# Expert sums and their layer norm in two halves, Gelu read from PSUM banks in the last feed-forward part, and one gather issued from ScalarE

## The chip, the cores and the metric

The kernel runs on one NeuronCore of a Trainium2 chip, in float32 throughout. A core has five engines with an instruction stream each: TensorE (PE; its weight loads are shown apart as PEld), VectorE (DVE), ScalarE (ACT), GpSimd (POOL) and SyncE (SP). Each works its stream in order; semaphores order the engines among themselves. The metric is the device time of one execution in microseconds.

## The reference

Two "metaformer" layers on x of shape (4 batches, 384 channels, 32 x 32 places), so 1024 tokens of 384 numbers for each batch.

```python
# layer 0
x = x + conv0(ln_c(x))        # selective scan: 4 directions, 384 channels, 16 states, 1024 steps
t = tokens(x); t = t + moe(ln_t(t))      # 4 experts 384 -> 1536 -> 384, the best 2 for each token
# layer 1
x = x + attention(ln_c(x))    # 8 heads of 64, queries = keys = values = w
t = tokens(x); t = t + ffn(ln_t(t))      # 384 -> 1536 -> 384, weights are Kronecker products
```

Every layer norm takes away a mean and divides by a root of a variance plus an epsilon. The experts and the feed-forward part (FFN) use Gelu between their two matrix products. A token's expert outputs are added with its two gate weights.

## The kernel before

The work falls into a *scan* (`scan_layer`) and a *tail* (`tail_batch`: experts, attention, FFN). The scan goes through the 4 batches; a batch has 8 units (4 directions x 2 halves of 512 steps), a unit has 3 chunks of 128 channels. In a chunk (`chunk`) DMAs bring `dtr` and `bcs`, POOL multiplies (line 440, and 468 for half of the results), ACT takes exponentials `da` (line 449), DVE runs the recurrences (line 454) and the other products (line 461), and PE sums over states into `acc` (line 475), 16 matmuls for each chunk. While the scan works on batch b+1, the tail of batch b runs between its instructions. After the last scan unit only tails are left: the rest of batch 2's and all of batch 3's.

The tail of a batch, in order:

- `route`/`spread`: tokens are transposed (`tt_ps`, 669), the gates computed (`places`), and each normalised token is written twice into `rows`, in an order sorted by expert, with 16 indirect DMAs from POOL (line 696, called puts here).
- `experts`: 11 slots, 8 of 256 rows and then 3 of 128. `fetch` loads weights, `gather` loads the slot's rows `xs` (line 935, which waits for the puts of the batch) and transposes them. Then `h_ps` (963), ACT adds the bias with Identity from the bank (968), one wide Gelu goes over all of `hs` (971), and PE makes `y_ps` (978), which DVE adds a bias to and a DMA stores into `made`.
- `combine`: POOL builds the diagonal gate matrices `diag` (999) and gathers each token's two results with 16 indirect DMAs (1008); PE weighs and adds them (`w_ps`, 1015) for 8 groups m of 128 tokens, and DVE adds the sum to `xt` (1018). One store writes all of `xt` (1019).
- `prologue`: bn_stats and bn_aggr on DVE for each m (543, 544), 1/root of the variance for all 8 on ACT (152, 153), `less` (552, 553), 8 normalisations on ACT (1031), and for each half of the tokens transposes (`tc_ps`, 1039) and copies (1043) to `xc`.
- `attention`: projection `w_ps` (1064), its copies (1067), transposes (1073, 1076), then scores `s_ps` (1087), exponentials (1093) and weighted sums `o_acc` (1133), and the division (`bc_ps`, 1109).
- `last_layers`: output projection `o_ps` (1185, 1187), layer norm (`x_mean`, `z_ps`, `x_var`; z in 152, 153 and 1216), and the FFN in `hidden`: 6 row-tiled matmuls `h_ps` on 32 rows (1231), copied from their banks (1237), one wide Gelu (1240), then 6 column-tiled matmuls `f_acc` (1248). Two calls of `hidden` make a half; then a copy `fy` (1253), three matmuls `fo_ps` (1256), three adds (1258) and three stores (1259).

`exp_again` (line 148) loads the table for exp and ln again after each wide Gelu; the load of Gelu's table is put in by the compiler ahead of it.

Order and places: the source gives dependencies and rough priorities (`high_priority`); the order of each engine's stream is made by a planner when the program is built, from its own estimate of times, and is fixed from then on. On the chip an engine that waits holds up all that stands behind it in its stream. Most DMAs are issued from SP's stream, the puts and the gathers of `combine` from POOL's, a few from ACT's. Memory comes from `Room`: tags with a number of buffers (`k4` has 5 beside the scan and 4 for batch 3; `k12` 2 and 3; `kw` 8 and 10), and PSUM banks "o" and "p" (1 and 3; for batch 3's second layer, `WIDE_BANKS`, 2 and 6). A new tile waits until the oldest of its tag is free.

Of the kernel before, what the change touches and what calls it, by code (L numbers as in the profile page):

```python
# [11 lines left out]
AF = mybir.ActivationFunctionType  # L12
# [5 lines left out]
P = 128  # L18
B = 4
D = 384  # L20
DC = D // P
HW = 32
L = HW * HW
HF = 512
NH = L // HF
# [12 lines left out]
FC = HID // P  # L38
# [7 lines left out]
NSLOT = NFULL + NHALF  # L46
# [5 lines left out]
MB = L // P  # L52
# [6 lines left out]
KR = 32  # L59
# [29 lines left out]
WIDE_BANKS = {"o": 2, "p": 6}  # L89
# [26 lines left out]
class Body:  # L116
# [389 lines left out]
    def first_layer(self, b, room):  # L506

        self.experts(b, self.slots, room)
        with self.tc.high_priority(offset=FORWARD):
            xt, xn = self.combine(b, *self.place, room)  # L510
            return self.prologue(xt, xn, room)

    def second_layer(self, b, xc, room, between):
        att = self.attention(xc, self.sums[:, b], room)
# [18 lines left out]

        return self.x2[b].rearrange("(m p) d -> p m d", p=P)

    def stats(self, xt, eps, room):

        nc = self.nc
        st = room.tile([P, MB, 6], "st", "st")
        mv = room.tile([P, MB, 2], "mv", "mv")  # L540
        rstd = room.tile([P, MB], "rstd", "rstd")
        for m in range(MB):
            nc.vector.bn_stats(st[:, m, :], xt[:, m, :])
            nc.vector.bn_aggr(mv[:, m, :], st[:, m, :])
        self.inverse_root(rstd, mv[:, :, 1], eps)
        return mv[:, :, 0], rstd

    def less_mean(self, mean, rstd, room, tag):

        less = room.tile([P, MB], tag, "less")  # L550
        ps = room.bank("p", "less_ps")[:, :MB]
        self.nc.scalar.copy(ps, rstd)
        self.nc.vector.scalar_tensor_tensor(less, mean, -1.0, ps, op0=ALU.mult, op1=ALU.mult)
        return less
# [338 lines left out]
    def experts(self, b, routed, room):  # L893
# [38 lines left out]
        def gather(s):  # L932
            at, size = extent(s)
            xs = room.tile([P, size // P, D], "k4", "xs")
            got = nc.sync.dma_start(
                out=xs, in_=rows[at : at + size, :].rearrange("(t p) d -> p t d", p=P)
            ).ins
            for put in placed:
                self.depend(got, put)
            xc = room.tile([P, DC, size], "k4", "xc")  # L940
            for lo in range(0, DC, HF // size):
                ps = room.bank("p", "xc_ps").rearrange("p (r l) -> p r l", l=size)
                n = min(HF // size, DC - lo)
                for c in range(lo, lo + n):
                    for t in range(size // P):
                        nc.tensor.transpose(  # L946
                            ps[:, c - lo, t * P : (t + 1) * P], xs[:, t, c * P : (c + 1) * P],
                            self.ident,
                        )
                nc.vector.tensor_copy(xc[:, lo : lo + n, :], ps[:, :n, :])  # L950
            return xc

        weights, xc = fetch(0), gather(0)
        for s in range(NSLOT):
            w1, w2, bb = weights
            at, size = extent(s)
            hs = room.tile([P, FC, size], "k12", "hs")
            n = HF // size
            for f in range(0, FC, n):
                ps = room.bank("p", "h_ps").rearrange("p (r l) -> p r l", l=size)  # L960
                for r in range(n):
                    for c in range(DC):
                        nc.tensor.matmul(  # L963
                            ps[:, r, :], w1[(f + r) // wf][:, c, (f + r) % wf * P : ((f + r) % wf + 1) * P],
                            xc[:, c, :], start=(c == 0), stop=(c == DC - 1),
                        )
                for r in range(n):
                    nc.scalar.activation(  # L968
                        hs[:, f + r, :], ps[:, r, :], AF.Identity, bias=bb[:, f + r : f + r + 1]
                    )  # L970
            self.exp_again(nc.scalar.activation(hs, hs, AF.Gelu).ins)  # L971
            if s + 1 < NSLOT:
                weights, xc = fetch(s + 1), gather(s + 1)
            y = room.tile([P, size // P, D], "k4", "y")
            for t in range(size // P):
                out = room.bank("o", "y_ps")
                for f in range(FC):
                    nc.tensor.matmul(  # L978
                        out[:, :D], hs[:, f, t * P : (t + 1) * P], w2[f // wf][:, f % wf, :],
                        start=(f == 0), stop=(f == FC - 1),  # L980
                    )
                nc.vector.tensor_add(y[:, t, :], out[:, :D], bb[:, FC:])  # L982

            queue = nc.sync if s + 1 < NSLOT else nc.scalar
            queue.dma_start(
                out=made[at : at + size, :].rearrange("(t p) d -> p t d", p=P), in_=y
            )

    def combine(self, b, pos, gate, room):
# [15 lines left out]
        for m in range(MB):  # L1005
            got.append(room.tile([P, TOP, D], "kw", "got"))
            for k in range(TOP):
# [4 lines left out]
        for m in range(MB):  # L1012
            ps = room.bank("p", "w_ps")[:, :D]
            for k in range(TOP):
                nc.tensor.matmul(
                    ps, diag[k][:, m, :], got[m][:, k, :], start=(k == 0), stop=(k == TOP - 1)
                )
            nc.vector.tensor_add(xt[:, m, :], xt[:, m, :], ps)
        nc.sync.dma_start(out=self.tokens(b), in_=xt)
        return xt, [got[m][:, 0, :] for m in range(MB)]  # L1020

    def prologue(self, xt, xn, room):


        nc = self.nc
        mean, rstd = self.stats(xt, self.eps6, room)
        less = self.less_mean(mean, rstd, room, "less")
        for m in range(MB):  # L1030
            nc.scalar.activation(
                xn[m], xt[:, m, :], AF.Identity, bias=less[:, m : m + 1], scale=rstd[:, m : m + 1]
            )
        xc = room.tile([P, DC, L], "k12", "xc")
        for i in range(NH):
            for c in range(DC):
                ps = room.bank("p", "tc_ps")
                for j in range(HF // P):
                    nc.tensor.transpose(
                        ps[:, j * P : (j + 1) * P], xn[i * (HF // P) + j][:, c * P : (c + 1) * P],  # L1040
                        self.ident,
                    )
                nc.scalar.copy(xc[:, c, halves(i)], ps)
        return xc
# [101 lines left out]
    def last_layers(self, b, att, room, between=()):  # L1146
# [24 lines left out]
        )  # L1171

        x2 = room.tile([P, DC, L], "k12", "x2")
        zs = []
        for i in range(NH):
            part = []
            for m in range(i * (HF // P), (i + 1) * (HF // P), 2):
# [36 lines left out]
            z = room.tile([P, HF], "k4", "z")  # L1214
            self.inverse_root(z, var, self.eps5, scale=1.0 / D)
            nc.vector.tensor_mul(z, z, zp)
            zs.append(z)
# [279 lines left out]
```

## Time and profile before

| what | us |
|---|---|
| median of 3 runs | 4267.21 (4253.81 to 4271.01) |
| the profiled execution, its own time | 4260.96 |
| its span, first to last instruction | 4258.3 |
| busy: PE, POOL, DVE, ACT | 3330.8, 3020.0, 2838.3, 2519.7 |
| last scan matmul (line 475) of batches 0, 1, 2, 3 ends at | 760, 1654, 2543, 3426 |
| first `h_ps` of the last FFN to the last add (1258) | 4187.8 to 4251.7 |

A timeline row holds start, duration, engine, line, operation, out<-in, shapes and count; in brackets stand the engine's idle time before it and what ended that. One float32 matmul leaves two records in PE's rows, so "x12" are 6 matmuls. A stretch's row holds its length, the busy time and count for each of PE, PEld, DVE, ACT and POOL, the granted share of PE's full clock, the busy share of the DMA engines, and GB/s.

### The profile page before, as it was taken

The numbers are of one execution on the slowest core, as the hardware profiler recorded it, in microseconds if no ns is written. First come the engines' busy times: TensorE is split into PE (matmuls) and PEld (weight loads), VectorE is DVE, ScalarE is ACT, GpSimd is POOL, SyncE is SP. The second block draws the span as 40 slices with busy tenths as digits, with TensorE's granted clock in tenths as the row PEclk, the third lists the DMA queues.
The fourth block names the chain that finished last, engine by engine and source line by source line (L and its number), as shares of the span: only waits on it lengthen the run. The fifth ranks groups of instructions, "written<-read, shape, count | busy, mean of one in ns | idle before, by whom it ended". The sixth has DMA issues, their size and how long they took to land. (4 is left out here: it accounts for less than half of the span.)

```text
span 4258.3 us, 45670 instructions
## 1 busy us (share of the span) xinstructions
PE 3330.8 (78%) x13308; PEld 1572.8 (37%) x13308; DVE 2838.3 (67%) x4148; ACT 2519.7 (59%) x4486; POOL 3020.0 (71%) x1471
## 2 busy tenths in 40 slices
PE   6445544389887888689996888679986899998896
PEld 2111101155553223255552223245553235666222
DVE  5999997788877877788877878778877830000101
ACT  5555545566665876666665776667664763443454
POOL 5999998898888977889989888879988830000100
PEclk8766666699998999699998999689997999999997
DMA  5554464678786534668887434668788343345100
GB/s 140 126 129 122 124 172 110 204 204 233 228 257 162 152 107 136 192 204 230 232 258 210 124 100 133 192 183 235 225 250 230 93 152 110 121 150 191 50 26 20
DMA packets 410322, 693.70 MB, mean 163 GB/s; under 512 B 51024, under 2 KB 209616, under 8 KB 410064
## 3 DMA queue, kind: packets, MB, share of 16 engines
q1 hardware_dynamic: 400752, 664.29, 54.3%
q0 software_dynamic: 8192, 25.17, 1.8%
q8 instruction: 107, 1.75, 0.2%
q14 instruction: 151, 1.24, 0.1%
q10 hardware_dynamic: 1120, 1.25, 0.1%
HBM read 569.00 MB, written 121.50 MB: 162 GB/s over the span
## 5 line engine op out<-in xcount | busy, mean ns | idle before, releaser
L440 POOL TENSOR_TENSOR bx<-dtr,bcs 128x1024 f32<-128x1024 f32 x768 | 1793.7, 2362 | 195.6 <-PE acc L475 84.0
L449 ACT ACTIVATE da<-dtr,nega 128x512 f32<-128x512 f32 x1536 | 1045.9, 690 | 898.8 <-DVE bx L461 551.1
L468 POOL TENSOR_TENSOR bx<-bx,bcs 128x1024 f32<-128x1024 f32 x384 | 905.4, 2362 | 132.4 <-DVE carry L465 59.9
L475 PE MATMUL acc<-bx,sel 128*32 128x512 f32 x3072 | 488.0, 691 | 309.8 <-POOL bx L468 282.2
L963 PE MATMUL h_ps<-xc,w 128*128 128x256 f32 (+1 forms) x3168 | 666.6, 365 | 65.6 <-DVE xc L950 28.3
L978 PE MATMUL y_ps<-w,hs 128*128 128x384 f32 x1824 | 643.7, 506 | 55.9 <-ACT hs L971 54.9
L963 PEld LDWEIGHTS h_ps<-xc,w 128*128 128x128 f32 x3168 | 551.9, 198 | 241.3 <-issue 124.5
L454 DVE TENSOR_TENSOR_SCAN bx<-da,carry,bx 128x512 f32<-128x512 f32 x384 | 473.7, 1271 | 134.5 <-POOL bx L440 69.5
L454 DVE TENSOR_TENSOR_SCAN bx<-da,bx 128x512 f32<-128x512 f32 x384 | 452.3, 1210 | 125.4 <-POOL bx L440 69.7
L454 DVE TENSOR_TENSOR_SCAN da<-da,carry,bx 128x512 f32<-128x512 f32 x384 | 475.7, 1274 | 79.5 <-ACT da L449 63.1
L461 DVE TENSOR_TENSOR bx<-da,bcs 128x512 f32<-128x512 f32 x768 | 509.6, 681 | 2.9
L454 DVE TENSOR_TENSOR_SCAN da<-da,bx 128x512 f32<-128x512 f32 x384 | 455.4, 1219 | 67.5 <-ACT da L449 46.8
L978 PEld LDWEIGHTS y_ps<-w,hs 128*128 128x128 f32 x1824 | 353.1, 197 | 338.5 <-issue 68.7
L1093 ACT ACTIVATE ex<-s_ps 128x512 f32<-128x512 f32 x512 | 300.2, 591 | 128.7 <-PE s_ps L1087 126.8
L1087 PE MATMUL s_ps<-w 64*128 64x512 f32 x1024 | 302.6, 653 | 70.1 <-ACT ex L1093 68.4
L968 ACT ACTIVATE hs<-h_ps,bb 128x256 f32<-128x256 f32 (+1 forms) x528 | 199.4, 441 | 220.0 <-PE h_ps L963 216.4
L999 POOL TENSOR_TENSOR diag<-ident,g_weight 128x1024 f32<-128x1024 f32 x8 | 15.0, 1898 | 419.9 <-PE xc_ps L946 406.4
L1133 PE MATMUL o_acc<-ex,vt 128*64 128x512 f32 x1024 | 281.9, 629 | 18.3 <-ACT ex L1093 14.7
L475 PEld LDWEIGHTS acc<-bx,sel 128*32 128x32 f32 x3072 | 75.0, 115 | 597.1 <-POOL bx L468 392.5
L982 DVE TENSOR_TENSOR y<-y_ps,bb 128x384 f32<-128x384 f32 x76 | 41.8, 550 | 223.4 <-PE y_ps L978 223.2
L1087 PEld LDWEIGHTS s_ps<-w 64*128 64x128 f32 x1024 | 80.6, 187 | 271.4 <-ACT ex L1093 222.7
L365 PE MATMUL dt_ps<-xd,wdt 108*128 108x512 f32 x192 | 123.7, 731 | 69.6 <-ACT mag L404 37.0
(213 smaller groups left out, 3611.4 us busy)
## 6 DMA issues: line engine op xcount, KB each, us to landing
w<-in_w SPq DMA_DIRECT2D x352, 576.0 KB
dtr<-dd SPq DMA_DIRECT2D x1536, 128.0 KB
bcs<-both SPq DMA_DIRECT2D x512, 128.0 KB
dd<-one_e SPq DMA_DIRECT2D x96, 256.0 KB
dd<-mag SPq DMA_DIRECT2D x96, 256.0 KB
rows<-zero SPq DMA_DIRECT2D x76, 192.0 KB
xt<-x SPq DMA_DIRECT2D x32, 384.0 KB
xs<-rows SPq DMA_DIRECT2D x32, 384.0 KB
```

The source lines that it names most:

```text
L440: pool = nc.gpsimd.tensor_mul(bx, dtr[q][1], bc[:, 0].unsqueeze(1).to_broadcast([P, 2, HF])).ins
L449: nc.scalar.activation(da, dtr[q][0][:, j, :], AF.Exp, scale=nega[:, col : col + 1])
L454: nc.vector.tensor_tensor_scan(run(h), run(da), run(bx[:, j, :]), 0.0 if first else hold, ALU.mult, ALU.add,)
L461: dve = nc.vector.tensor_mul(bx[:, j, :], h, cg).ins
L468: pool = nc.gpsimd.tensor_mul(bx, bx, cg.unsqueeze(1).to_broadcast([P, 2, HF])).ins
L475: nc.tensor.matmul(acc[lo : lo + DB, :], sel, out[q][:, j, :], start=(g == 0), stop=(g == NG - 1),)
L963: nc.tensor.matmul(ps[:, r, :], w1[(f + r) // wf][:, c, (f + r) % wf * P : ((f + r) % wf + 1) * P], xc[:, c, :], start=(c == 0), stop=(c = ...
L968: nc.scalar.activation(hs[:, f + r, :], ps[:, r, :], AF.Identity, bias=bb[:, f + r : f + r + 1])
L978: nc.tensor.matmul(out[:, :D], hs[:, f, t * P : (t + 1) * P], w2[f // wf][:, f % wf, :], start=(f == 0), stop=(f == FC - 1),)
L1087: ins = nc.tensor.matmul(ps, w[rows, j * P : (j + 1) * P], w[rows, halves(i)], start=True, stop=True).ins
L1093: done.append(nc.scalar.activation(ex[:, o, :], ps, AF.Exp, scale=HD**-0.5, accum_out=sums[:, t, 2 * j + o, i : i + 1],).ins)
L1133: ins = nc.tensor.matmul(out[cols, :], made[t][1][:, j, cols], ex[:, o, :], start=(j == 0), stop=(j == MB - 1),).ins
```

## The change

Five edits.

1. `combine` no longer makes all 8 sums. It returns a function `add(m)`, which `prologue` calls for the four groups of a half, with their statistics, inverse root, `less` and normalisations; then come this half's transposes and copies, and then the second half. The store of `xt` is split in two. `less` takes its PSUM bank from tag "o" in `prologue`. (`stats` goes; `second_layer_exact`, a branch for overflow that is not taken with these inputs, uses `prologue` without `add`.)
2. In the last of the 11 slots the wide Gelu covers `hs` without the last group of 4 rows and is tied to a matmul near the end of that group (the first of its last row); the last group's rows get Gelu straight from their bank, with the bias.
3. In batch 3's FFN (`alone`: the room with `WIDE_BANKS`) `quickly` takes the place of `hidden`: 4 matmuls into 4 banks and 4 Gelus straight from them, three calls for each half, without copies, a wide Gelu or `exp_again`.
4. The first slot's rows are loaded from ACT's stream instead of SP's.
5. Both halves of z lie in one `k4` tile instead of two.

```diff
     def first_layer(self, b, room):
             self.experts(b, self.slots, room)
             with self.tc.high_priority(offset=FORWARD):
-                xt, xn = self.combine(b, *self.place, room)
-                return self.prologue(xt, xn, room)
+                xt, xn, add = self.combine(b, *self.place, room)
+                return self.prologue(xt, xn, room, add)
...
         def gather(s):
-            got = nc.sync.dma_start(
+            queue = nc.scalar if s == 0 else nc.sync
+            got = queue.dma_start(
...
             for f in range(0, FC, n):
+                last = s == NSLOT - 1 and f == FC - n
...
+                        if last and r == n - 1 and c == 0:
+                            wide = nc.scalar.activation(hs[:, :f, :], hs[:, :f, :], AF.Gelu).ins
+                            self.depend(wide, ins)
                 for r in range(n):
-                    nc.scalar.activation(
-                        hs[:, f + r, :], ps[:, r, :], AF.Identity, bias=bb[:, f + r : f + r + 1]
-                    )
-            self.exp_again(nc.scalar.activation(hs, hs, AF.Gelu).ins)
+                    done = nc.scalar.activation(
+                        hs[:, f + r, :], ps[:, r, :], AF.Gelu if last else AF.Identity,
+                        bias=bb[:, f + r : f + r + 1],
+                    ).ins
+            if not last:
+                done = nc.scalar.activation(hs, hs, AF.Gelu).ins
+            self.exp_again(done)
...
-        for m in range(MB):
+        def add(m):
             ps = room.bank("p", "w_ps")[:, :D]
...
             nc.vector.tensor_add(xt[:, m, :], xt[:, m, :], ps)
-        nc.sync.dma_start(out=self.tokens(b), in_=xt)
-        return xt, [got[m][:, 0, :] for m in range(MB)]
+            if m % (MB // NH) == MB // NH - 1:
+                part = slice(m + 1 - MB // NH, m + 1)
+                nc.sync.dma_start(out=self.tokens(b)[:, part, :], in_=xt[:, part, :])
+        return xt, [got[m][:, 0, :] for m in range(MB)], add
...
-    def prologue(self, xt, xn, room):
+    def prologue(self, xt, xn, room, add=lambda m: None):
...
         for i in range(NH):
+            st = room.tile([P, nh, 6], f"st{i}", "st")
+            mv = room.tile([P, nh, 2], f"mv{i}", "mv")
+            rstd = room.tile([P, nh], f"rstd{i}", "rstd")
+            for j in range(nh):
+                m = i * nh + j
+                add(m)
+                nc.vector.bn_stats(st[:, j, :], xt[:, m, :])
+                nc.vector.bn_aggr(mv[:, j, :], st[:, j, :])
+            self.inverse_root(rstd, mv[:, :, 1], self.eps6)
+            less = self.less_mean(mv[:, :, 0], rstd, room, f"less{i}", "o")
+            for j in range(nh):
+                m = i * nh + j
+                nc.scalar.activation(
+                    xn[m], xt[:, m, :], AF.Identity, bias=less[:, j : j + 1], scale=rstd[:, j : j + 1]
+                )
...
-        zs = []
+        zt = room.tile([P, NH, HF], "k4", "z")
+        zs = [zt[:, i, :] for i in range(NH)]
...
-        ng = 6
+        alone = room.banks is WIDE_BANKS
+        ng = nq if alone else 6
+
+        def quickly(i, at):
+            hs = room.tile([P, ng, HF], "k12", "hs")
+            banks = [room.bank("p", "h_ps") for _ in range(nq)]
+            for o, ps in enumerate(banks):
+                rows = slice(o * KR, (o + 1) * KR)
+                nc.tensor.matmul(
+                    ps, fc1[rows, at // nq, :], zs[i][rows, :], start=True, stop=True
+                )
+            for o, ps in enumerate(banks):
+                nc.scalar.activation(hs[:, o, :], ps, AF.Gelu)
+            return hs
 
         def hidden(i, at):
+            if alone:
+                return quickly(i, at)
```

More of the change, by code (lines that the diff above doesn't have):

```diff
@@ L534, in tokens, with less_mean @@
         return self.x2[b].rearrange("(m p) d -> p m d", p=P)
[L536 to L541, printed above, removed]
-        for m in range(MB):
[L543 to L551, printed above, removed]
+    def less_mean(self, mean, rstd, room, tag, bank="p"):
+        n = rstd.shape[-1]
+        less = room.tile([P, n], tag, "less")
+        ps = room.bank(bank, "less_ps")[:, :n]
         self.nc.scalar.copy(ps, rstd)
@@ L962, in experts @@
                     for c in range(DC):
[L963 removed]
+                        ins = nc.tensor.matmul(
                             ps[:, r, :], w1[(f + r) // wf][:, c, (f + r) % wf * P : ((f + r) % wf + 1) * P],
                             xc[:, c, :], start=(c == 0), stop=(c == DC - 1),
[L966 removed]
+                        ).ins
+                        if last and r == n - 1 and c == 0:
+                            wide = nc.scalar.activation(hs[:, :f, :], hs[:, :f, :], AF.Gelu).ins
+                            self.depend(wide, ins)
                 for r in range(n):
[L968 to L971 removed]
+                    done = nc.scalar.activation(
+                        hs[:, f + r, :], ps[:, r, :], AF.Gelu if last else AF.Identity,
+                        bias=bb[:, f + r : f + r + 1],
+                    ).ins
+            if not last:
+                done = nc.scalar.activation(hs, hs, AF.Gelu).ins
+            self.exp_again(done)
             if s + 1 < NSLOT:
@@ L1011, in combine @@
                 )
-        for m in range(MB):
+        def add(m):
             ps = room.bank("p", "w_ps")[:, :D]
@@ L1018, in combine @@
             nc.vector.tensor_add(xt[:, m, :], xt[:, m, :], ps)
-        nc.sync.dma_start(out=self.tokens(b), in_=xt)
-        return xt, [got[m][:, 0, :] for m in range(MB)]
-    def prologue(self, xt, xn, room):
-        nc = self.nc
[L1028 to L1034, printed above, removed]
-        for i in range(NH):
+            if m % (MB // NH) == MB // NH - 1:
[3 more added lines that the diff above has]
+    def prologue(self, xt, xn, room, add=lambda m: None):
+        nc = self.nc
+        nh = MB // NH
+        xc = None
+        for i in range(NH):
+            st = room.tile([P, nh, 6], f"st{i}", "st")
[13 more added lines that the diff above has]
+                )
+            if xc is None:
+                xc = room.tile([P, DC, L], "k12", "xc")
             for c in range(DC):
@@ L1213, in last_layers @@
                 nc.tensor.matmul(var, self.ones, sq[:, c, :], start=(c == 0), stop=(c == DC - 1))
-            z = room.tile([P, HF], "k4", "z")
+            z = zs[i]
             self.inverse_root(z, var, self.eps5, scale=1.0 / D)
             nc.vector.tensor_mul(z, z, zp)
-            zs.append(z)
         for step in between:
             step()
-        ng = 6
+        alone = room.banks is WIDE_BANKS
[11 more added lines that the diff above has]
+            return hs
         def hidden(i, at):
+            if alone:
+                return quickly(i, at)
             hs = room.tile([P, ng, HF], "k12", "hs")
```

## The prediction

> **What bounds the kernel now.** I began with the page's table of forty slices, because a kernel in stages has no single bound.
>
> ```profile
> PE   6445544389887888689996888679986899998896
> POOL 5999998898888977889989888879988830000100
> PEclk8766666699998999699998999689997999999997
> ```
>
> For 33 slices POOL (the scan's products) is at eight or nine tenths; then it falls to 0 and PE alone carries the last fifth. So time can be won in two places under different rules: in the interleaved part only if the scan gets on faster, at the end by anything that shortens PE's waits. The table of stretches, cut where the last scan matmul (line 475) of a batch ends, gives the sizes (columns: length; busy time of PE, PEld, DVE, ACT, POOL; clock; DMA):
>
> ```profile
> 760.00:1654.00 894.00, 728.33 (x3070) 356.97 (x3067) 709.20 (x1023) 584.17 (x1074) 781.16 (x382) 0.90 0.66 190
> 1654.00:2543.00 889.00, 735.75 (x3023) 362.17 (x3021) 693.48 (x1010) 595.65 (x1042) 757.63 (x371) 0.90 0.66 192
> 2543.00:3426.00 883.00, 732.03 (x3040) 363.71 (x3037) 699.99 (x1013) 579.90 (x1003) 758.66 (x369) 0.90 0.65 187
> 3426.00:4258.30 832.30, 755.36 (x3051) 385.67 (x3047) 87.03 (x214) 362.25 (x749) 38.38 (x37) 0.95 0.31 105
> ```
>
> The last row is 832.3 us with PE busy for 755: here PE's waits are the time. The timeline of the end shows its largest, in the last feed-forward part:
>
> ```profile
> 4193.94 1.07 ACT L1237 COPY hs<-h_ps 128x512 f32<-128x512 f32 x2 [0.72 <-PE h_ps L1231]
> 4195.03 1.28 ACT L1240 ACT_TABLE_LOAD   x1
> 4196.33 2.76 ACT L1240 ACTIVATE hs<-hs 128x3072 f32<-128x3072 f32 x1
> 4199.14 3.55 PE L1248 MATMUL f_acc<-hs,wc 128*32 128x512 f32 x12 [5.22 <-ACT hs L1240]
> 4215.26 4.96 PE L1256 MATMUL fo_ps<-fy,wc 128*128 128x512 f32 x6 [0.85 <-DVE fy L1253]
> 4251.00 0.69 DVE L1258 TENSOR_TENSOR out<-fo_ps,x 128x512 f32<-128x512 f32 x1 [0.46 <-PE fo_ps L1256]
> ```
>
> PE stands 5.2 us before each of four groups of f_acc (four `hidden` calls) while ACT copies, loads a table and runs one wide Gelu.
>
> **The change, part by part.** The sum runs against the profiled execution: 4260.96 us (span 4258.3), which is 6.25 under the median of 4267.21.
>
> *Gelu from banks (last batch alone).* Before: 24 copies, 4 wide Gelus of 2.77, 8 table loads of 1.28. After: 24 Gelus from banks and 4 loads. No Gelu from a bank is in the trace; nearest is the exp from a bank, same shape (591 ns mean, 0.58 start to start); the wide Gelu's 2.76 for six rows argues for no more. The built order interleaves on PE: h_ps x4, x_var x2, then f and h in turn, most singly. Singles are priced by attention, where row-tiled s_ps and column-tiled o_acc alternate in the same way:
>
> ```profile
> 4133.29 1.13 PE L1087 MATMUL s_ps<-w 64*128 64x512 f32 x4
> 4134.35 1.08 PE L1133 MATMUL o_acc<-ex,vt 128*64 128x512 f32 x4
> 4135.36 1.13 PE L1087 MATMUL s_ps<-w 64*128 64x512 f32 x4
> ```
>
> That is 2.07 us for two bursts, 1.035 each. A rule here speaks against the change: the Trainium skill ("TensorE: Matmul & The Clock Gate", the table "Why this matters for your kernels") says that a matmul on 32 rows takes as long as a full one, and that what is won comes from running several at once. Read from the code alone (four h in a row, four f in a row) a half would need 6 bursts, 6.2 us; by the built order half 0 has 14 after x_var and half 1 has 16, where before a half had about 10. I take the order's count. Then:
> - x_var ends at 4190.9, as before. 14 bursts: 4205.4. ACT keeps ahead: the Gelu load follows the last square (4187.9), four Gelus end at 4191.6; then load, Ln 0.69, load, Exp 0.63, load (3 x 1.28 + 1.32 = 5.2) for z's second half, 4196.8. The next f that needs a Gelu is burst 9, at 4199.2, 1.8 us after the fifth Gelu is done.
> - fy and its gaps 0.83 (before: 4214.43 to 4215.26); three fo at 0.89 (line 1064: 12 records, 6 matmuls, 5.32): 4209.0.
> - h for half 1 stands behind fo in the order, so ACT idles and the second half can't overlap. 16 bursts: 4225.6. fy, fo and the last add: 4230.1.
>
> Before, that add ended at 4251.69: a gain of 21.6. It needs the full clock. The stretches give 1.00 in the first row and half under the Gelu waits:
>
> ```profile
> 4186.00:4190.00 4.00, 3.41 (x10) 1.23 (x10) 1.26 (x3) 2.83 (x5) 0.00 (x0) 1.00 0.00 0
> 4207.00:4211.00 4.00, 0.22 (x4) 0.20 (x8) 0.00 (x0) 3.97 (x3) 0.00 (x0) 0.50 0.00 0
> 4211.00:4215.00 4.00, 3.41 (x12) 0.37 (x4) 0.49 (x1) 1.03 (x1) 0.00 (x0) 0.50 0.02 4
> ```
>
> The same page (Part 1) has the clock halve after an idle window of about 3.4 us and recover after as long of work. The new order has no PE wait over 1.4 us, so by that rule the clock stays full: 21.6. The rows alone allow the pessimist's reading, that this stage is always cold: fo at 1.65 (4.96 for three) is 1.85 times the 0.89, 30 bursts would cost 26 more and six fo 4.6 more, a loss of 9. I stay near the rule, as attention's alternation ran at 1.00, and allow one half-speed window, 2 us: **-19.5** (ends -21.6 and +9).
>
> *Halves of the sums.* Last batch:
>
> ```profile
> 3967.34 0.55 DVE L1018 TENSOR_TENSOR xt<-xt,w_ps 128x384 f32<-128x384 f32 x1 [1.17 <-PE w_ps L1015]
> 3969.77 4.89 ACT L1031 ACTIVATE got<-xt,less,rstd 128x384 f32<-128x384 f32 x8 [0.28 <-DVE less L553]
> 3974.57 2.96 ACT L1043 COPY xc<-tc_ps 128x512 f32<-128x512 f32 x6
> 3976.63 5.32 PE L1064 MATMUL w_ps<-xc,wqkv 128*128 128x512 f32 x12
> ```
>
> The gathers keep their pace (POOL, 16 x 1.26 us), so the last add stays. Behind it are four norms (2.45) in place of eight; their transposes end 0.5 later, at 3972.7, and the projection starts with three matmuls of half 0 (2.7 us), which hide half 1's three copies (1.8). Start 3972.7 for 3976.63: **-3.9**. The first half's transposes stand on PE ahead of w_ps 4 to 7 and cost those about 2 us; three w_ps of 0.89 catch up before the last gather (3966.3). If they didn't, 2 us come back. The second store and the second set of rstd, less and copy (0.30 + 0.21 + 0.17) lie inside the gathers.
>
> *Last slot's Gelu.*
>
> ```profile
> 3927.95 1.48 ACT L971 ACTIVATE hs<-hs 128x1536 f32<-128x1536 f32 x1
> 3929.49 9.65 PE L978 MATMUL y_ps<-w,hs 128*128 128x384 f32 x24 [4.03 <-ACT hs L971]
> ```
>
> In the built program the load waits for the first matmul of the last row, some 0.45 before h ends; load 1.28 and 1024 elements at about 1.04 let y_ps begin 1.9 after h ends, and its first eight matmuls (3.2) hide four Gelus of 0.29. 4.03 becomes 1.9: **-2.1**. A warmer clock could add 1.7, as y_ps without a wait took 7.91.
>
> *In batches 0 to 2* the same edits meet a scan that sets the time. ACT gets two more loads in batches 1 and 2 (exps stand between the Gelus): 4 x 1.28 = 5.1 us, on an engine 65% busy. What hides them is ACT's own waiting (551 us for DVE at line 449). Uncovered they cost 5. The planner also deals the tail anew among the scan's matmuls, mostly within half a chunk of the old place; after the last scan matmul PE holds the same 1585 instructions in both. How much dealing matters, the first table tells: three batches, dealt differently, took 894, 889 and 883. I take **0**, from -12 to +20.
>
> *First gather on ACT* leaves SP's stream (where it stood behind out stores and weights) and stands among ACT's exps: in batches 0 to 2 behind exps that ended at about 858, 1835 and 2797 before; SP issued it at 859, 1823 and 2793. The last puts ended on POOL at 845.8, 1783.3 and 2756.7 and land in at most 7.9, so ACT should find them done, and pays 0.33 of issue each (as line 985 from ACT): **0**. In batch 3 it comes 2.3 us before the landing at 3508.4; attention's exps wait that long, and PE waited 2.65 for these rows anyway. *z in one tile* frees a buffer and moves no instruction: **0**.
>
> Sum: -19.5 - 3.9 - 2.1 = -25.5. 4235.5 for the profiled execution, 4241.7 at the median's level.
>
> **The rivals.** *The end stays cold or PE-bound:* half of the windows at half speed cost 15 of the 19.5: 4257. For it: more bursts than before, half clock now. Against: no long wait is left. *The middle gives back what the end wins:* about 7 us per batch, inside the spread seen between batches: 4262. *The middle wins too* (shorter prologues, 4 us each): 4230. *Slower, by one mechanism:* the gather blocks ACT. Behind it stand 6 to 9 exps per batch; DVE and then POOL follow at once, so each us of waiting is a us of scan. Batch 0 has only 4 us to spare (845.8 + 7.9 against 858), the others 32 and more. It decides once the waits add up to over 25.5; 45 would give 4287. *The edits do nothing,* as the scheduler undoes them: excluded by the built order, save for z and the gather.
>
> **How the numbers follow.** About 0.5% (21 us) is what a measurement of this kernel can tell from no change: the three runs span 17. That bound is 4245.9. The forecast gets 0.55, own range 4230 to 4254, nearly three quarters of it under the bound: 0.40 faster, 0.15 same. The middle winning: 0.12, faster. Cold end 0.15 and middle slipping 0.10: same. Gather 0.08: slower. Together 0.52, 0.40, 0.08. The range reaches down to the middle's gain with a warm end, 4220, and up past the slipping middle to 4270.
>
> **What would show it.** Right: the four 5.2 us waits gone, and some 43 us from the first h_ps to the last add (63.9 before, from 4187.8 to 4251.7); clock near 1.00 in that stretch; four norms between the last add and the projection; y_ps 2 us after h. Wrong: f_acc rows at half clock, exps (line 449) waiting for puts, or batches of the scan that differ from 883 to 894 by more than 12; the last alone could turn the sign.

## The result and the profile after

The changed kernel takes 4244.2 us (median of 14 runs, 4230.7 to 4256.2) where the kernel before, run beside it, takes 4264.4 (14 runs, 4253.8 to 4271.1). The ratio is 0.9957, 95% interval 0.9947 to 0.9968: 18 us less (14 to 23), 0.43% (the two medians alone differ by 20). That is just inside the 0.5% which I had called no change. The forecast was 4241.7 with a range of 4220 to 4270.

The profiled execution of the changed kernel took 4230.72 us (span 4228.9). It was the shortest of its 14, so single stages can be read from it, but not what is typical of the first three batches.

The page's forty slices after the change; each digit is a tenth of busy time, or of the clock:

```profile
PE   6544545489897888789996888789996899999898
POOL 5999997898988978789899878889897840000100
PEclk8666666589998999789997999789997899999999
```

The shape is the same: POOL busy for 32 slices, mostly at seven to nine tenths, then PE alone. In the last slice PEclk is at nine tenths where before it was at seven.

The stretches, cut again where the last scan matmul (line 475) of a batch ends. Columns: length; busy time of PE, PEld, DVE, ACT, POOL; clock; DMA share and GB/s:

```profile
761.00:1637.00 876.00, 714.95 (x2977) 348.06 (x2973) 696.81 (x999) 577.25 (x1064) 767.39 (x376) 0.89 0.66 191
1637.00:2541.00 904.00, 756.90 (x3125) 373.74 (x3125) 715.24 (x1043) 605.32 (x1064) 771.94 (x378) 0.91 0.66 190
2541.00:3418.00 877.00, 743.68 (x3029) 365.76 (x3025) 698.21 (x1006) 577.50 (x1003) 757.16 (x368) 0.89 0.65 188
3418.00:4228.90 810.90, 758.60 (x3051) 387.47 (x3047) 86.96 (x215) 347.06 (x744) 38.39 (x37) 0.97 0.32 108
```

The last row fell from 832.3 to 810.9 us while PE's busy time stayed (755 and 759): PE stands still less. The first three rows were 894, 889 and 883; now they are 876, 904 and 877. The prediction had named batches more than 12 us away from 883 to 894 as a sign against it. They are at most 10 away, though a single row moved by as much as 18.

The timeline of the last feed-forward part after the change (start, length, engine, line, operation; in brackets the idle time before it and what ended it):

```profile
4177.78 1.14 PE L1243 MATMUL h_ps<-z,wc 32*128 32x512 f32 x8
4181.26 1.28 ACT L152 ACT_TABLE_LOAD   x1
4185.20 1.28 ACT L1247 ACT_TABLE_LOAD   x1
4186.84 1.04 PE L1276 MATMUL f_acc<-hs,wc 128*32 128x512 f32 x2
4187.82 1.13 PE L1243 MATMUL h_ps<-z,wc 32*128 32x512 f32 x6
4195.66 2.84 PE L1284 MATMUL fo_ps<-fy,wc 128*128 128x512 f32 x6 [0.82 <-DVE fy L1281]
4210.68 1.12 PE L1243 MATMUL h_ps<-z,wc 32*128 32x512 f32 x2
4211.73 1.05 PE L1276 MATMUL f_acc<-hs,wc 128*32 128x512 f32 x2
4219.37 0.69 DVE L1286 TENSOR_TENSOR out<-fo_ps,x 128x512 f32<-128x512 f32 x1 [0.17 <-PE fo_ps L1284]
```

The four waits of 5.2 us are gone. h and f take turns, a pair in 2.03 us (f at 4186.84, the next one at 4188.88). From the first h_ps to the end of the last add it is 42.28 us (4177.78 to 4220.06), where before took 63.86.

### The profile page after: what moved, and what is told of

Read it like the earlier page. It is cut to its first block, busy times and chain, and to the rows that moved or that the text cites. A ratio compares the mean times of both kernels' runs of the same rounds, so it can differ in the third digit from the quotient of the medians.

```text
span 4228.9 us, 45721 instructions
## 1 busy us (share of the span) xinstructions
PE 3363.3 (80%) x13308; PEld 1581.4 (37%) x13308; DVE 2846.4 (67%) x4152; ACT 2505.9 (59%) x4494; POOL 3020.1 (71%) x1471
## 4 chain that ended last, share of the span: by engine, by line
PE 37%; DVE 22%; ACT 11%; DMA 11%; POOL 9%; issue 7%; SPq 3%; DVEq 0%; POOLq 0%; ACTq 0%
PE y_ps L975 9%; PE h_ps L954 9%; DVE da L454 8%; DVE bx L454 7%; POOL bx L440 5%; DMA dtr<-dd 4%; ACT da L449 3%; PE s_ps L1099 3%; PE acc L475 3%; DVE bx L461 3%; PE o_acc L1145 3%; POOL bx L468 2%; DMA w<-in_w 2%; SPq L424 2%; DMA bcs<-both 1%
## 5 line engine op out<-in xcount | busy, mean ns | idle before, releaser
L475 PE MATMUL acc<-bx,sel 128*32 128x512 f32 x3072 | 500.2, 697 | 294.0 <-POOL bx L468 256.8
L954 PE MATMUL h_ps<-xc,w 128*128 128x256 f32 (+1 forms) x3168 | 675.8, 370 | 71.0 <-DMA w<-in_w 40.0
L975 PE MATMUL y_ps<-w,hs 128*128 128x384 f32 x1824 | 634.4, 500 | 26.7 <-ACT hs L967 20.1
L954 PEld LDWEIGHTS h_ps<-xc,w 128*128 128x128 f32 x3168 | 561.0, 201 | 240.7 <-issue 120.2
```

Of the source, the lines that this page charges most:

```text
L475: nc.tensor.matmul(acc[lo : lo + DB, :], sel, out[q][:, j, :], start=(g == 0), stop=(g == NG - 1),)
L954: ins = nc.tensor.matmul(ps[:, r, :], w1[(f + r) // wf][:, c, (f + r) % wf * P : ((f + r) % wf + 1) * P], xc[:, c, :], start=(c == 0), sto ...
L975: nc.tensor.matmul(out[:, :D], hs[:, f, t * P : (t + 1) * P], w2[f // wf][:, f % wf, :], start=(f == 0), stop=(f == FC - 1),)
```

## The experiments

Twelve kernels were run, each timed in five rounds beside the kernel before. The last four ran in a session in which the kernel before took 4293.6 us instead of 4262, so ratios are compared, and lengths within a trace. "In us" is the ratio times the time of before.

### One edit of the change, in its place

**e1: Gelu from banks alone.** The kernel before with the `quickly` part of the diff; the order of everything ahead of it is that of before.

```diff
+        alone = room.banks is WIDE_BANKS
+        ng = nq if alone else 6
...
         def hidden(i, at):
+            if alone:
+                return quickly(i, at)
```

> The kernel before with one edit, Gelu from banks in the last feed-forward part; every other instruction stands where it stood before. Theory A (the whole gain is PE's waits in the last feed-forward part): 42.3 us from the first h_ps to the last add where before took 63.9, so -21.6 us, ratio 0.995. Rival B (the scan's part of the span won what the medians show): about 0 us, ratio 1.000. Rival C (the Gelus from banks are quick only because something earlier had warmed the clock): the stretch takes 50 us or more and the clock falls under 1.00 in it; -14 us or less, ratio 0.997.

Measured: ratio 0.9945 (0.9929 to 0.9960), -23 us (-30 to -17). The stretch takes 42.23 us. The clock is 1.00 in every 4 us from 4176 to 4228. So the stretch is quick without the other edits (B and C fall), and this one edit alone carries all that the whole change won, and rather more.

**e2: everything but that edit.** The changed kernel with copies and wide Gelus in the last feed-forward part.

```diff
-        alone = room.banks is WIDE_BANKS
-        ng = nq if alone else 6
+        ng = 6
...
-            if alone:
-                return quickly(i, at)
```

> The changed kernel with the last feed-forward part put back to copies and wide Gelus; the order up to there is that of the changed kernel. Theory A: what is left of the change is -3.6 us at the last slot, -0.4 us at the halves and a give-back of some 5 us over batches 0 to 2, so +1 us, ratio 1.000 (0.999 to 1.002). My prediction's own terms: -3.9 -2.1 +0 = -6 us, ratio 0.9986. Rival B (the gain lies ahead of the last feed-forward part): -20 us, ratio 0.995.

Measured: 1.0014 (1.0005 to 1.0024), +6 us (+2 to +10). The other four edits together cost time; with e1's -23 that makes -17, against -18 for the whole change. Its profiled execution is near its median (4267.37 and 4267.99), so its first three batches may be read:

```profile
758.70:1639.60 880.90, 716.38 (x2973) 351.79 (x2973) 694.45 (x999) 577.38 (x1064) 767.24 (x376) 0.89 0.65 190
1639.60:2549.40 909.80, 760.15 (x3127) 374.15 (x3129) 721.29 (x1043) 606.00 (x1066) 772.63 (x378) 0.91 0.65 189
2549.40:3432.00 882.60, 747.32 (x3027) 364.75 (x3027) 699.04 (x1006) 576.70 (x1001) 756.70 (x368) 0.89 0.64 187
```

The scan ends at 3432.0 where it ended at 3426.2 before: about 6 us given back, 21 lost in the second row and 13 won in the first. Behind the scan the slot and the halves win 4, but the old feed-forward part took 67.8 us here in place of 63.9 (why, is told under "not expected"), and the stretch behind the last add 9.2 in place of 6.6 (see e7).

**e3: the last slot's Gelu from the bank, in batch 3 alone.**

```diff
+                last = b == B - 1 and s == NSLOT - 1 and f == FC - n
...
+                        if last and r == n - 1 and c == 0:
+                            wide = nc.scalar.activation(hs[:, :f, :], hs[:, :f, :], AF.Gelu).ins
+                            self.depend(wide, ins)
```

> The kernel before with the last slot's Gelu taken from the bank in batch 3 alone; the order up to that slot is that of before. Theory A: the wait ahead of the last y_ps falls from 4.03 to 2.04 us, and the 24 matmuls of y_ps take 8.0 in place of 9.65 us because the clock has less time to fall: -3.6 us, ratio 0.9992. As predicted: the wait alone, -2.1 us, y_ps still about 9.6 us. Rival (the gathers that follow wait for the stores of y anyway): the wait falls but the first gather comes no earlier, 0 us.

Measured: 0.9998 (0.9986 to 1.0010), which can't tell -3.6 us from nothing. The trace can. First e1, where this stage is as before, then e3:

```profile
3926.47 1.48 ACT L971 ACTIVATE hs<-hs 128x1536 f32<-128x1536 f32 x1
3928.00 9.70 PE L978 MATMUL y_ps<-w,hs 128*128 128x384 f32 x24 [4.03 <-ACT hs L971]
```

```profile
3925.02 1.06 ACT L969 ACTIVATE hs<-hs 128x1024 f32<-128x1024 f32 x1
3925.99 1.13 ACT L972 ACTIVATE hs<-h_ps,bb 128x128 f32<-128x128 f32 x4
3926.13 8.01 PE L985 MATMUL y_ps<-w,hs 128*128 128x384 f32 x24 [2.04 <-ACT hs L969]
```

The wait went from 4.03 to 2.04, and the 24 matmuls behind it from 9.70 to 8.01: the end of y_ps moved from 3937.70 to 3934.14, and the first combining gather with it (3941.1 and 3937.6). The faster matmuls are the clock: it stood at 1.00 for all of e3's, and at half for the first 3.4 us of e1's. The changed kernel shows the same two numbers. Only the first half of the gain is sure: in e8 below, the same wait of 2.04 was followed by 9.70.

**e4: the sums in halves, in batch 3 alone.**

```diff
         with self.tc.high_priority(offset=FORWARD):
+            if b == B - 1:
+                xt, xn, add = self.combine_halves(b, *self.place, room)
+                return self.prologue_halves(xt, xn, room, add)
```

> The kernel before with the sums in halves in batch 3 alone. As predicted: from the first combining gather to the first s_ps of attention 36.7 us where before took 40.6, so -3.9 us. Theory A (the second half's w_ps stand behind the first half's transposes and cannot catch up, and the projection runs at a lower clock): last add 27.2 us behind the first gather instead of 25.3, projection 6.8 us instead of 5.3, in all -0.4 us, ratio 1.000. Which of the two losses is tied to the edit itself is told by the clock of the projection: at 1.00 here the second loss was chance and the sum is -1.9 us.

Measured: 1.0011 (1.0003 to 1.0019), +5 us (+1 to +8). From the first combining gather to the first s_ps of attention it is 39.96 us where before had 40.64: the prediction's -3.9 is not there. The rest of the +5 lies in the last feed-forward part, 67.7 us as in e2. The place in e4:

```profile
3962.96 2.82 PE L1115 MATMUL tc_ps<-ident,got 128*128 128x128 f32 x12 [3.20 <-ACT got L1107]
3966.03 5.53 PE L1054 MATMUL w_ps<-got,diag 128*128 128x384 f32 x16 [0.25 <-ACT xc L1119]
3971.60 0.56 DVE L1057 TENSOR_TENSOR xt<-xt,w_ps 128x384 f32<-128x384 f32 x1
3974.77 2.70 PE L1115 MATMUL tc_ps<-ident,got 128*128 128x128 f32 x12 [3.21 <-ACT got L1107]
3977.26 6.64 PE L1140 MATMUL w_ps<-xc,wqkv 128*128 128x512 f32 x12
```

The second half's sums (line 1054) wait behind the first half's transposes and then for ACT's copies of them, and come in one run of 5.5 us. DVE follows with an add and its statistics per 1.29 us, so the last add ends 26.95 us behind the first gather (25.33 before). Then the projection takes 6.64 us for work that took 5.32. Both losses are also in the changed kernel (27.17 and 6.78).

### Where the halves went

**e6: the first half's transposes behind all sums.** As e4, with

```diff
+                    if i == 0:
+                        self.depend(ins, self.summed)
```

where `self.summed` is the last sum's matmul.

> Sums in halves in batch 3 alone as in e4_last_halves_only, but the first half's transposes stand behind the last w_ps of the second half on PE. Theory A (the halves lost 1.9 us because the transposes held up the second half's sums, and 1.3 us because PE came to the projection with a halved clock after 3.2 us of standing still): the last add is 25.4 us behind the first gather (26.9 in e4), the projection takes 5.3 us (6.6 in e4), first gather to first s_ps 38.9 us (40.0 in e4, 40.6 before): -1.7 us on before, ratio 0.9996, about what a measurement can tell from nothing, so read from the trace. Rival (the lower clock of the projection was chance, or comes from PE having less to do in halves): the projection stays at 6.6 us.

Measured: 1.0007 (0.9997 to 1.0017); the span in question 39.99 us, last add 26.75, projection 6.43. Theory A failed twice. The transposes were out of the way, and yet the sums were late:

```profile
3961.34 0.88 PE L1054 MATMUL w_ps<-got,diag 128*128 128x384 f32 x2 [0.75 <-DVE less L557]
3964.52 5.06 PE L1054 MATMUL w_ps<-got,diag 128*128 128x384 f32 x10 [2.29 <-DMA got<-made,g_pos]
```

PE now waited 2.29 us for gathered rows. The stretches of 2 us in which these rows were under way (columns as above):

```profile
3959.42:3961.42 2.00, 0.99 (x3) 0.40 (x3) 0.83 (x4) 0.75 (x4) 1.55 (x2) 1.00 0.95 270
3961.42:3963.42 2.00, 0.81 (x2) 0.19 (x2) 0.54 (x2) 2.00 (x4) 1.53 (x2) 1.00 1.05 343
```

The DMA engines are full, at a time when the gathers alone keep them half busy. What fills them, by its time and size, is the store of the first half, 768 KB issued at 3959; e9 tests that. And the projection stayed at 6.4, the clock at half from 3974.5 to 3977.9: its cold clock did not come from the order of the transposes.

**e9: as e6, with one store at the end.**

```diff
-            if m % (MB // NH) == MB // NH - 1:
-                part = slice(m + 1 - MB // NH, m + 1)
-                nc.sync.dma_start(out=self.tokens(b)[:, part, :], in_=xt[:, part, :])
+            if m == MB - 1:
+                nc.sync.dma_start(out=self.tokens(b), in_=xt)
```

> As e6_last_halves_tied, but the sums of batch 3 are stored once, after the last of them, and not half by half. Theory D (in e6 the second half's sums were late because the first half's store, 768 KB in the midst of the gathers, filled the DMA engines for 4 us and held the gathered rows up, PE waiting 2.3 us for them): that wait is gone, the DMA share stays near 0.5 until the last gather, and the last add is 25.4 us behind the first gather (26.2 in e6, 27.0 in e4); first gather to first s_ps about 39.2 us. Rival (the gathers were late in e6 for another reason, the order of their own packets): the wait of 2.3 us is still there. The projection should again take 6.4 to 6.6 us, since PE again stands still just ahead of the second half's transposes; if it takes 5.3, the store had to do with that too.

Measured: 0.9999 (0.9987 to 1.0011). The wait of 2.3 us is gone, and the same stretch looks like this:

```profile
3984.10:3986.10 2.00, 1.44 (x4) 0.30 (x2) 0.86 (x3) 2.00 (x4) 1.47 (x2) 1.00 0.55 148
3986.10:3988.10 2.00, 1.67 (x4) 0.59 (x4) 0.99 (x3) 0.43 (x1) 1.39 (x2) 1.00 0.58 174
```

The last add ends 25.32 us behind the first gather, as before the change, and first gather to first s_ps is 38.31: 2.3 less than before, and 0.9 better than expected. Theory D holds. The projection still takes 6.18. In e11 below, with the same order, it took 5.32, and the span was 37.18, 3.5 less than before. So the halves can be worth nearly the predicted 3.9; it takes the sums ahead of the transposes, one store, and luck with the clock.

### What batches 0 to 2 gave back

**e7: both halves of z in one tile, and nothing else.**

```diff
-        zs = []
+        zt = room.tile([P, NH, HF], "k4", "z")
+        zs = [zt[:, i, :] for i in range(NH)]
...
-            z = room.tile([P, HF], "k4", "z")
+            z = zs[i]
```

> The kernel before with both halves of z in one tile and nothing else. As predicted (it moves no instruction that counts): 0 us, ratio 1.000. Theory B (the 6 us that batches 0 to 2 lost in the changed kernel come from the dealing of the tail's work among the scan's matmuls, which any edit of tiles deals anew): no work is added, yet the ends of the batches' scans shift by several us either way, ratio off 1.000 by up to 0.002, sign not foretold. Theory C (those 6 us are the price of the edits' own work, loads and stores): 1.000 here.

Measured: 1.0008 (0.9998 to 1.0018), +3 us (-1 to +8). The stretches of its batches:

```profile
756.80:1656.60 899.80, 728.95 (x3070) 358.34 (x3067) 710.11 (x1023) 583.99 (x1074) 780.68 (x381) 0.90 0.65 188
1656.60:2563.60 907.00, 745.17 (x3057) 361.74 (x3059) 694.27 (x1013) 597.63 (x1050) 758.26 (x371) 0.89 0.65 188
2563.60:3429.30 865.70, 726.15 (x2985) 357.01 (x2985) 699.03 (x1010) 570.79 (x985) 758.14 (x369) 0.90 0.66 191
```

No work was added, and the second batch became 18 us longer and the third 17 shorter than before. So which tail work lies among which batch's scan is dealt anew by an edit of one tile, and a single row of this table says nothing about an edit. In kernels whose order up to the tail is that of before (e1, e3 to e6) the rows nearly repeat, 898 to 903, 884 to 887 and 879 to 884 (before itself: 894, 889 and 883).

This trace also shows a price at the very end. The last add:

```profile
4260.70 0.69 DVE L1258 TENSOR_TENSOR out<-fo_ps,x 128x512 f32<-128x512 f32 x1 [0.47 <-PE fo_ps L1256]
```

From its end at 4261.4 to the end of the span at 4270.4 are 9.0 us; in the changed kernel 8.9 (4220.06 to 4228.9), in e2 9.2. These are the three kernels with z in one tile. In the eleven others that stretch takes 6.6 to 6.8 us. So the edit goes with 2.3 us more there; by what path is open.

**e8: the last slot's Gelu in all batches.**

```diff
-                last = b == B - 1 and s == NSLOT - 1 and f == FC - n
+                last = s == NSLOT - 1 and f == FC - n
```

> The kernel before with the last slot's Gelu from the bank in all four batches, as the change has it. Theory C (two more table loads in each of batches 1 and 2 are paid by the scan): 4 x 1.28 = +5 us in the middle, -3.6 us at batch 3's slot, +1.5 us in all, ratio 1.0003, and the scans of batches 1 and 2 end later by 2.6 us each. Theory B (dealing): the scans' ends move by more than 2.6 us or the other way. As predicted (hidden): middle 0, -2 to -3.6 us, ratio 0.999.

Measured: 1.0018 (1.0006 to 1.0031), +8 us (+3 to +13), where e3, the same edit in batch 3 alone, had -1 (-6 to +4). That does not yet show a cost in batches 0 to 2. Behind the scan both kernels do the same work, and there too e8's profile is the longer one, by 8.5 us: y_ps 9.70 for 8.01, first combining gather to first s_ps 43.48 for 40.60, feed-forward part 68.0 for 64.1. In y_ps the mean clock was 0.82 where e3 had 1.00. The lengths of e8's batches (896, 896 and 894) come from the longest of its 14 executions, 15 us above its median, and can't be set against others.

What the trace does show is 104 table loads between the ends of the batches' scans, where before had 96: the exps of scan and attention fall between the Gelus more often than I had counted, 8 loads more where I had four. That is 8 x 1.28 = 10 us of ACT's time; whether the scan pays for it is not shown. The changed kernel and e2 have 100 loads there; 4 x 1.28 = 5.1.

**e10: the first slot's rows on ScalarE's queue, and nothing else.**

```diff
-            got = nc.sync.dma_start(
+            queue = nc.scalar if s == 0 else nc.sync
+            got = queue.dma_start(
```

> The kernel before with the first slot's rows loaded from ScalarE's queue and nothing else. As predicted (ACT finds the puts landed and pays 0.33 us of issue in each of the first three batches): 0 us, no exp of the scan waits for a put. Rival of the prediction (the gather blocks ACT): exps of the scan wait for the puts, tens of us, ratio 1.004 or more. Theory B (dealing): lengths of the three batches differ from 894, 889 and 883 by several us in either direction, with no wait for a put.

Measured: 0.9986 (0.9977 to 0.9996), -6 us (-10 to -2). The trace shows the four issues on ACT at 0.37 to 0.42 us and no idle time ahead of any; in the changed kernel too (0.37 to 0.44). The rival by which this edit could have turned the sign is dead. Where the 6 us come from I can't say: the profiled execution was the longest of its 22, so its rows can't be set against the others.

**e12: the halves in all four batches.**

```diff
-            xt, xn = self.combine(b, *self.place, room)
-            return self.prologue(xt, xn, room)
+            xt, xn, add = self.combine(b, *self.place, room)
+            return self.prologue(xt, xn, room, add)
```

> The kernel before with the sums in halves in all four batches, as the change has it, and nothing else. Theory B (dealing, no work of the edit's own): the lengths of the three batches move by several us in either direction, their sum within 10 us of before's 2666, ratio 0.998 to 1.002. Theory E (in batches 0 to 2 the halves shorten the prologue by some 4 us each, as a rival of the prediction had it): sum of the three lengths 12 us less, ratio 0.997. Theory C (the second store and norms are paid by the scan): sum several us more, ratio 1.002.

Measured: 1.0000 (0.9988 to 1.0012). The three batches together take 2682 us; e9, of the same session and with before's order up to the tail, takes 2681. The profile's tail behind them is 10 us longer than e9's (847.9 and 837.5), so these sums alone decide nothing. The ratio does: neither E's gain (0.997) nor C's price (1.002) lies in its interval.

### Can it be beaten?

**e5: the last feed-forward part in steps of three.** The edit puts a new function in the place of the loop, for batch 3:

```diff
+        for n, (i, at) in enumerate(steps):
+            if n + 1 < len(steps):
+                made.append(hidden(*steps[n + 1], made[n - 1][1][-1] if n > 0 else rooted))
...
+            for f in range(at, at + ng):
+                ins = nc.tensor.matmul(
+                    out[f % nq * KR : (f % nq + 1) * KR, :], pj1[:, f, :], hs[:, f - at, :],
+                    start=(f < nq), stop=(f >= FC - nq),
+                ).ins
+                if f == at:
+                    self.depend(ins, done[-1])
```

`hidden` makes three h_ps in three banks and three Gelus from them; `rooted` is the Exp of the second z.

> The kernel before with its last feed-forward part written in steps of three: three h_ps in one burst, three Gelus from banks, three f_acc in one burst, the next step's h ahead of this step's f, six banks in turn. Theory A (in the changed kernel that stage is bound by the count of its bursts on PE, about 1.03 us each whether one matmul or four run in them): 16 bursts at 1.1 = 17.6, six fo_ps at 0.89 = 5.3, two fy with their gaps 1.6, and some 4 us until the first Gelus are there: about 29 us from the first h_ps to the last add, where before took 63.9 and the changed kernel 42.3; -34 us on before, ratio 0.992. Rival (what bounds it there is the Gelus, 24 at 0.58 with their loads, or the number of matmuls whatever the burst): about 42 us again, -22 us, ratio 0.995.

Measured: 0.9937 (0.9920 to 0.9954), -27 us. The part takes 36.78 us, neither 29 nor 42. Its timeline:

```profile
4194.23 1.14 PE L1275 MATMUL h_ps<-z,wc 32*128 32x512 f32 x8 [3.43 <-ACT z L1216]
4198.00 2.08 PE L1275 MATMUL h_ps<-z,wc 32*128 32x512 f32 x4
4216.25 1.14 PE L1275 MATMUL h_ps<-z,wc 32*128 32x512 f32 x6
4217.31 1.06 PE L1293 MATMUL f_acc<-hs,wc 128*32 128x512 f32 x6
4220.21 0.69 DVE L1302 COPY fy<-f_acc 128x512 f32<-128x512 f32 x1 [7.00 <-PE f_acc L1293]
```

Where the clock is up, a burst of three matmuls costs 1.06 to 1.14, no more than a single one. Behind the first half's fo_ps, nine h and nine f, six bursts, run with their waits from 4212.41 to 4220.21: 0.87 us for an h and an f, where the changed kernel, mostly with single ones, needs 1.44 (twelve of each from 4198.44 to 4215.7). So the changed kernel's part is bound by the count of its bursts. What I missed is ahead of that: two Gelus got in front of the second z's Ln, so that tables were loaded three more times and PE waited 3.43 us, and then the bursts cost 1.93 to 2.08 each at half clock until 4205.9.

**e11: that, mended, with the last slot's Gelu and the halves of e9, in batch 3 alone.**

```diff
-        self.depend(made[0][1][0], rooted)
+        for gelu in made[0][1]:
+            self.depend(gelu, rooted)
...
-                made.append(hidden(*steps[n + 1], made[n - 1][1][-1] if n > 0 else rooted))
+                made.append(hidden(*steps[n + 1], made[n - 1][1][-1] if n > 0 else None))
```

> A candidate to beat both: the kernel before with the steps of three of e5_grouped_ffn in the last feed-forward part, all its Gelus behind the Exp of the second z (so that the tables are loaded once), the last slot's Gelu of e3_last_slot_only and the halves of e9_halves_one_store, in batch 3 alone; the order up to batch 3's last slot is that of before. Sum: the feed-forward part 34 to 35 us in place of 63.9 (36.8 in e5, less 1 us at the start and about as much at its waits), -29; slot -3.6; halves -1; in all -33 to -34 us on before, ratio 0.992. It fails if the wait for the second z before the first Gelu costs more than the two table loads that it saves, or if the halved clock behind that wait lasts longer than the 4 us seen in e5: then -27 to -30 us, ratio 0.9935.

Measured: 0.9913 (0.9896 to 0.9930), -37 us (-45 to -30). By the trace: feed-forward part 33.08 (-30.8), slot -3.6, halves -3.5, sum -37.9. It beats before, and by intervals that don't meet also the changed kernel (0.9947 to 0.9968 in its own comparison):

```profile
4213.70 0.63 ACT L1299 ACTIVATE z<-z 128x512 f32<-128x512 f32 x1
4214.34 1.28 ACT L1364 ACT_TABLE_LOAD   x1
4217.34 1.62 PE L1377 MATMUL f_acc<-hs,wc 128*32 128x512 f32 x6
4218.88 2.08 PE L1358 MATMUL h_ps<-z,wc 32*128 32x512 f32 x6
4221.97 1.13 PE L1358 MATMUL h_ps<-z,wc 32*128 32x512 f32 x6
```

One table load, and half clock for some three bursts only.

## Why the prediction was right, and where it was not

The sum came out at 4241.7 against 4244.2. It was right for its largest term and owes the rest to errors that cancel: the Gelus and the slot won 3.6 us more than forecast, the halves 3.5 less. The nearness of the two totals is luck in part: 25.5 us less than the 4264.4 that the kernel before took beside the changed one would be 4238.9, and the forecast started from 4267.2. By the bound of 0.5% what came is "within 0.5%" (chance 0.40) and not "faster" (0.52), by 3 us.

1. *Gelu from banks, -19.5.* Worked out as -21.6, measured -21.58, and shown by e1 to be this edit's own. Counting bursts by the built order and pricing each by attention's rows was the right step: 2.03 us a pair for the predicted 2.07. The 2 us set aside for one cold window were not needed. The Trainium skill ("TensorE: Matmul & The Clock Gate", Part 1) decided rightly against the pessimist's reading: the longest wait of PE in the new stretch is 0.82 us, and the clock stayed at 1.00.

2. *Halves, -3.9.* Measured -0.4 in the changed kernel and -0.7 in e4. Two steps failed. "Three w_ps of 0.89 catch up before the last gather": PE could, but only after it had the transposes and ACT's copies behind it, and then DVE could not, which needs 1.29 us for each sum with its statistics. "The second store ... inside the gathers" was costed at nothing without naming what it takes: the DMA engines, which the gathers were using. With the transposes moved it cost 1.4 us (26.75 to 25.32 from e6 to e9); in the changed kernel it lay behind the transposes' delay. The last add to the start of the projection shrank as foretold, from 8.7 to 5.0 us. A third loss was in no step: with only 12 transposes behind the last wait of PE, the half clock fell on the projection (6.8 us for 5.3; 3964.6 to 3968.0), where before it fell on the transposes (3970.4 to 3973.8), which waited for ACT anyway. It need not come: e11 has the wait and no half clock.

3. *Last slot, -2.1.* Measured -3.6: -2.0 from the wait, as worked out, and -1.6 from y_ps at a warmer clock, the term that I had named ("could add 1.7") and left out of the sum. It is not firm: 8.01 us in the changed kernel, e2, e3 and e11, 9.70 in e8.

4. *Batches 0 to 2, 0.* The tail's parts add up to -21.6 - 3.6 - 0.4 = -25.6, and the measured change is -18 (-23 to -14): about 7 us came back. Some 2.3 of them lie behind the last add (point 5). The other 5 (0 to 9) should lie in the middle: in e2, with the same order up to the end, the scan ended 6 us later. (In the changed kernel's own profile, the shortest of its 14, it ended 8 earlier.) The step that probably failed is "what hides them is ACT's own waiting": 551 us of waiting for DVE in total do not tell whether ACT waits just where a load falls. That the loads are the cause is not shown, as e8 can't tell. The dealing, which I had taken as spread alone, is the rival: with no work added it moved single batches by 18 us and their sum by 6 (e7).

5. *Gather on ACT, 0*: it never waited, as argued from the times of the last puts. Yet alone it measured -6 us (-10 to -2), which no step foretold and no trace explains. *z in one tile* was called an edit that "moves no instruction"; e7 shows that it deals the middle anew, and the three traces that have it show 2.3 us more behind the last add. The measured time, +3 us (-1 to +8), can tell that neither from 0 nor from more.

Of the rivals, the middle gave back as one of them said, but some 5 us over three batches and not 7 in each; the cold end, the winning middle and the blocking gather did not come.

## What to carry to other kernels

Price a chain of small matmuls by its bursts in the built order, not by its matmuls: one and three or four that run at once cost the same 1.05 to 1.14 us here, so after the waits are gone, grouping them is the next gain. When a phase is cut in halves, ask for each shared engine what of the second half now stands behind the first, the store's DMA traffic included; and of an edit that is repeated in a stage bound by something else, try first the copy that lies on the serial end alone (e11 has its edits in the last batch only, and its -37 agrees with the -37.9 of its stages).

## What was not expected of the hardware

The old feed-forward part, with the same instructions in the same order, took 63.8 to 64.1 us in six profiles (before, e3, e7, e9, e10 and e12) and 67.6 to 68.0 in four (e2, e4, e6, e8). The difference lies in where the half-speed spells fall. In e2 the clock is at half from 4224.6 to 4255.3 without a break. That catches the last three groups of h_ps, which in the profile of before take 1.13 or 1.14 each; here are the last two:

```profile
4232.40 3.63 PE L1260 MATMUL f_acc<-hs,wc 128*32 128x512 f32 x12 [5.22 <-ACT hs L1252]
4235.96 2.08 PE L1243 MATMUL h_ps<-z,wc 32*128 32x512 f32 x4
4238.70 2.08 PE L1243 MATMUL h_ps<-z,wc 32*128 32x512 f32 x4 [0.67 <-ACT hs L1249]
```

So waits of 5.2 us made not only idle time but a spread of 4 us, more than the slot's edit won; the changed kernel is rid of both. There is one profile of each kernel, so whether the kernel or the single execution decides is not shown. But the four kernels also measured +3 to +8 us against before, the other five -6 to +3.

A wait of PE need not be long to cost clock: in e6 one of 2.34 us (3970.89 to 3973.23) was followed by half clock from 3974.5 to 3977.9. The Trainium skill ("TensorE: Matmul & The Clock Gate", Part 1) speaks of an idle window of about 3.4 us; here less was enough. And it need not cost clock: in e11 the same wait (2.34 us, up to 3996.50) left it at 1.00. Nor is recovery always quick: in e5 PE worked without a gap from 4196.1 on and the clock stayed at 0.50 until 4205.9, while in e11 the same kind of bursts had it back after 3.4 us (4217.7 to 4221.1). These spells last 3.4, 10.2 and 3.4 us, one step or three of the same length. So it may decide where a wait falls against such a step; no run tests that, and what makes the difference is open.
